# Group norms with one late product, the first output's weights by identity products, and a last image with its own buffers

## The chip, the core and the metric

The kernel runs on one core of a Trainium2 chip. Its time is the device time of one execution in microseconds (us), the median of the runs shown; lower is better. The engines are named as in the profile: PE is TensorE, DVE is VectorE, ACT is ScalarE, POOL is GpSimd, SP is SyncE. Each engine has its own queue and takes its instructions strictly in order; between engines semaphores do the ordering.

## What is computed

```python
def reference(x, ...):                      # x: 16 images, 128 channels, 64 x 64
    x = x + conv(gn(x), g_pos, g_neg, bias, input_factor, output_factor)
    x = x + attention_free(gn(x), Wq, Wk, Wv, B, Wm)
    return x

def conv(x, ...):
    v = round(clip(x * input_factor, -1, 1) * 127) / 127 * 0.6
    v = pad(swap the last two axes of v)
    fv = patches3x3(v + 0.1 * v ** 3)
    outs = [fv @ (g_pos - g_neg)[i] for i in range(3)]
    y = adc(outs[2]) + 4 adc(outs[0]) + 2 adc(outs[1]) + adc(outs[2])
    return y * output_factor + bias

def attention_free(x, ...):                 # 64 inner channels
    q, k, v = Wq x, Wk x, Wv x
    return Wm (q * (exp(B) (exp(k) v)) / (exp(B) exp(k)))

def gn(v):                                  # 32 groups of 4 channels, over the whole image
    return (v - mean) / sqrt(var + 1e-5)
```

Everything is float32; `adc` rounds to an integer and clips.

## The kernel before

**Work.** Channels lie on the 128 partitions, one image after the other. The 3x3 convolution goes through a transformed domain: DVE forms transformed rows of the quantized image (`gr`, `er`, `pa`, `pb`, `cs`, `cq`, `cd`, `p0`, `p5`, `e0`, `e5`), PE multiplies them with transformed weights, ACT and DVE carry the results back. Each image has three outputs (i = 0, 1, 2, the three weight planes), each in two halves, so there are six half-blocks, .0 to .5. A half-block holds eight products of `Block.half` (`q1`, `q2`, `q0`, `q3` for two points u) and later five of `Block.rest` (`P`, two in each of `o0` and `o1`). Between them stand ACT copies out of PSUM: `m1` (L579) before `q2`, `sd` (L581) before `q0` and `q3`, `sA` (L584) after `q0`. DVE adds with `Bo`, `df`, `sm`, `ma`, `mc`, `S0`, `S3` and `bc` (L625), ACT rounds with `tk` (L633), DVE clips with `bA`/`bB` (L636), and a POOL DMA adds the output into the integer tile `acc` with `aA`/`aB` (L643).

**The second layer.** Class `End` makes the residual: ACT writes `acc` times a scale with a row sum (`cx0` to `cx3`, L699), POOL DMAs add the input image onto it (`cd0x` to `cd3x`, L702), ACT squares with a row sum (`sq0` to `sq3`, L364). Then comes the group norm, and four `Pair`s of 1024 columns: normalize (`xn`), three projections (`kp`, `vp`, `qp`), `ek`, `ekv`, the mixing product `dn`, a reciprocal (`g`, `u`, `ln`, `ex`), `oa`, `ob`, `oc`, the output product `op`, `r`, a POOL DMA adding the residual (`rd`, L812) and the store (`st`, L813). The pairs' normalized tile and their output `r` share two buffers `xns`.

**Group norm** (class `Norm`). Per image there is one for the input (name x) and one for the residual (name y). Per channel it takes a sum and a sum of squares about a shift, which `shift` (L357 or L360) makes from the channel's own first quarter. `begin` (L368 to L378) makes the channel's mean and spread, `means` multiplies the mean with a group-averaging matrix `grp2` on PE (L383), `squares` (L387 to L389) adds what the channel's mean differs from the group's, `variances` averages again on PE (L392), and `guess`, `root`, `finish` make 1/sqrt. That is two products that depend on each other, both after the last square.

**Weights.** In the first 20 us the three weight planes are loaded as g_neg, negated (`W0a` to `W2a`, L313) and g_pos added by POOL DMAs (`W0A` to `W2A`, L240). Then each plane is transformed into `us` by fifteen small DVE and ACT operations (`Wic` to `Wip`, L316 to L333).

**Order.** The order on all five queues is written out in lists of names: `FIRST` for the start and the first two images, `ORDER` once per turn for the middle images (a turn holds the convolution of image p and the second layer of images p-1 and p-2; "+1" means the work belongs to the turn before), and `LAST` for the last two images. The names are the keys of the dictionaries that `operations` returns.

**The last image.** `Last` finishes half-blocks .4 and .5 of image 15: `tP`, `tp`/`to` are the products (into `pb` and `py`), `tbc`/`tbd` DVE sums in PSUM (L625), `tk0`/`tk3` ACT roundings (L633), `tb` clips, `ta` additions into `acc` (L684). The input image is loaded by SP into `x2e` (L717), and `tx` (L724) makes acc times scale plus input with row sums, `ts` (L364) the squares; then the norm and four `LastPair`s with buffers of their own.

Of the kernel before, what the change touches and what calls it, by code (L numbers as in the profile page):

```python
# [30 lines left out]
EPS = 1e-5  # L31

RECIP = float(0x7EF311C7)
RSQRT = float(0x5F3759DF)
# [28 lines left out]
    hs0+2 x0+2 hq0+2 hs1+2 hq1+2 hq2+2 hq3+2 W0a+2 W0A+2 hs2+2 hs3+2 xa+2 W1a+2 pmx+2 xb+2  # L63
    pvx+2 W2a+2 xc+2 xl+2 hi+2 xd+2 W0b+2 W0c+2 hn1+2 hn0+2 W0e+2 W2A+2 hc0+2 hc1+2 W0d+2 W0f+2
    hn3+2 W2f+2 li0+1 hc3+2 hr1+2 hv1+2 hr0+2 hv0+2 li1+1 W2c+2 W0j+2 er0+2 hn2+2 W0g+2 W1A+2
    sx0+1 sx1+1 W0i+2 gr0+2 W0J+2 cp+2 W0k+2 hc2+2 hr3+2 W1c+2 W0h+2 W1b+2 x0+1 hr2+2 hv3+2
    W1e+2 W1J+2 hv2+2 W0n+2 W0l+2 hb+2 er1+2 sy1+1 W1f+2 gr1+2 W1j+2 li3+1 W0m+2 W0p+2 W0o+2
    pb1+2 hz1+2 hz0+2 sy0+1 li2+1 sx2+1 sy2+1 hcs1+2 hcs0+2 q11.0+1 hcq1+2 hcq0+2 pa1+2 sx3+1
    q10.0+1 sy3+1 m11.0+1 xa+1 W1d+2 W2b+2 hcd0+2 q21.0+1 cs1+2 m10.0+1 W1g+2 q20.0+1 sd0.0+1
    sd1.0+1 W2d+2 hcd1+2 lj0+1 W1h+2 q01.0+1 q30.0+1 q00.0+1 W2e+2 W2g+2 W1i+2 sA1.0+1 cd1+2  # L70
    sA0.0+1 pmx+1 W2h+2 q31.0+1 q11.1+1 m11.1+1 xb+1 cq1+2 q10.1+1 W1l+2 m10.1+1 q21.1+1 lj1+1
    Bo.0+1 W2J+2 pvx+1 W2j+2 q20.1+1 sd0.1+1 q00.1+1 sd1.1+1 q01.1+1 W1k+2 q30.1+1 df.0+1 xc+1
    W1m+2 q31.1+1 p0+1 xl+1 W1o+2 W1n+2 xd+1 sA0.1+1 e0+1 n1+1 P.2+1 sm.0+1 q10.2+1 W1p+2 W2i+2
    Bo.1+1 W2l+2 n0+1 sA1.1+1 df.1+1 q11.2+1 m10.2+1 q20.2+1 sd0.2+1 cl0+1 q00.2+1 sm.1+1
    m11.2+1 ma.2+1 q21.2+1 sA0.2+1 sd1.2+1 q10.3+1 mc.2+1 q01.2+1 p5+1 s0+1 cl1+1 S0.2+1
    q30.2+1 q31.2+1 va0+1 s1+1 S3.2+1 sA1.2+1 lj3+1 W2m+2 q11.3+1 W2n+2 m10.3+1 Bo.2+1 bc.2+1
    m11.3+1 q20.3+1 bA.2+1 va1+1 df.2+1 q21.3+1 lj2+1 e5+1 sd0.3+1 sd1.3+1 n3+1 o1.2+1 n2+1
    o0.2+1 q00.3+1 gr0+1 q30.3+1 q31.3+1 sA0.3+1 q01.3+1 tk.2+1 P.3+1 W2p+2 li0+0 er0+1 sA1.3+1
    W2o+2 q10.4+1 Bo.3+1 sm.2+1 cp+1 bc.3+1 df.3+1 q11.4+1 m11.4+1 o0.3+1 cl2+1 cl3+1 W2k+2
    sx0+0 sm.3+1 s2+1 va2+1 mc.4+1 ma.4+1 q21.4+1 m10.4+1 q20.4+1 sd0.4+1 o1.3+1 sd1.4+1 S0.4+1  # L80
    aA.2+1 x0+0 q30.4+1 li1+0 tk.3+1 S3.4+1 q00.4+1 sA0.4+1 q31.4+1 P.4+1 bc.4+1 s3+1 q01.4+1
    q10.5+1 Bo.4+1 o1.4+1 bB.3+1 va3+1 sx1+0 bA.4+1 er1+1 m10.5+1 q20.5+1 sA1.4+1 aA.4+1 sy1+0
    q11.5+1 m11.5+1 o0.4+1 gr1+1 sd0.5+1 li3+0 tk.4+1 sy0+0 q21.5+1 P.5+1 q00.5+1 sd1.5+1
    q01.5+1 df.4+1 pb0+1 sA1.5+1 q30.5+1 sA0.5+1 q31.5+1 bc.5+1 pa0+1 o1.5+1 Bo.5+1 cq0+1
    df.5+1 cs0+1 o0.5+1 li2+0 tk.5+1 P.0+0 q10.0+0 sm.4+1 m10.0+0 q11.0+0 m11.0+0 sm.5+1
    q20.0+0 sd0.0+0 q21.0+0 sd1.0+0 cd0+1 q01.0+0 mc.0+0 aB.3+1 S0.0+0 bB.5+1 bc.0+0 sx2+0
    pa1+1 ma.0+0 pb1+1 q00.0+0 sA0.0+0 q30.0+0 o0.0+0 S3.0+0 o1.0+0 sy2+0 q31.0+0 aB.5+1 cs1+1
    sx3+0 sy3+0 bA.0+0 aA.0+0 tk.0+0 P.1+0 sA1.0+0 q11.1+0 q10.1+0 m10.1+0 lj1+0 bc.1+0 o0.1+0
    Bo.0+0 m11.1+0 cq1+1 lj0+0 xa+0 o1.1+0 tk.1+0 cd1+1 bB.1+0 aB.1+0 q20.1+0 sd0.1+0 pmx+0
    xb+0 ho+2 q21.1+0 p5+0 sd1.1+0 q00.1+0 pvx+0 xc+0 q01.1+0 p0+0 sA0.1+0 df.0+0 q10.2+0  # L90
    sA1.1+0 q11.2+0 q30.1+0 xl+0 q31.1+0 m10.2+0 q20.2+0 m11.2+0 e5+0 e0+0 cx0+0 Bo.1+0 y0+0
    cx1+0 sm.0+0 cx2+0 sd0.2+0 df.1+0 cd0x+0 cx3+0 q21.2+0 cd1x+0 cd2x+0 q00.2+0 xd+0 sd1.2+0
    sm.1+0 mc.2+0 q01.2+0 sA0.2+0 n1+0 n0+0 q30.2+0 ma.2+0 sq0+0 cd3x+0 S0.2+0
"""
START = "x0 xa pmx xb pvx xc xl xd gr0 er0 cp gr1 er1 pb1 pa1 cs1 cq1 cd1"

LAST = """
    cl0+2 sA1.2+2 S3.2+2 q31.2+2 lj3+2 st2+2 q10.3+2 cl1+2 P.2+2 bc.2+2 m10.3+2 q11.3+2 m11.3+2
    s0+2 q20.3+2 q21.3+2 o0.2+2 Bo.2+2 va0+2 s1+2 va1+2 sd0.3+2 o1.2+2 bA.2+2 sd1.3+2 q01.3+2
    sq1+2 sq2+2 lj2+2 gr0+2 sq3+2 q30.3+2 q00.3+2 tk.2+2 sA1.3+2 er0+2 q31.3+2 sA0.3+2 ya+2  # L100
    df.2+2 n3+2 n2+2 pmy+2 yb+2 P.3+2 bc.3+2 Bo.3+2 cp+2 q11.4+2 pvy+2 q10.4+2 yc+2 cl3+2
    df.3+2 o0.3+2 m10.4+2 m11.4+2 o1.3+2 q20.4+2 q21.4+2 yl+2 s3+2 yd+2 xn0+2 sd0.4+2 sd1.4+2
    kp0+2 vp0+2 sm.3+2 tk.3+2 P.4+2 q01.4+2 cl2+2 sm.2+2 ek0+2 va3+2 mc.4+2 s2+2 st3+2 aA.2+2
    S0.4+2 ekv0+2 bc.4+2 dn0+2 sA1.4+2 g0+2 q00.4+2 sA0.4+2 va2+2 u0+2 xn1+2 ln0+2 o1.4+2 gr1+2
    o0.4+2 q30.4+2 oa0+2 ex0+2 kp1+2 er1+2 tk.4+2 qp0+2 ob0+2 vp1+2 q11.5+2 ma.4+2 oc0+2 S3.4+2
    ek1+2 m11.5+2 pb0+2 op0+2 r0+2 ekv1+2 q31.4+2 Bo.4+2 rd0+2 q10.5+2 pa0+2 m10.5+2 st0+2
    P.5+2 q20.5+2 df.4+2 bc.5+2 sd0.5+2 q21.5+2 sd1.5+2 dn1+2 q00.5+2 g1+2 bB.3+2 xn2+1 bA.4+2
    q01.5+2 q30.5+2 o1.5+2 o0.5+2 u1+2 cs0+2 oa1+2 ln1+2 cd0+2 q31.5+2 ex1+2 tk.5+2 sA1.5+2
    sA0.5+2 cq0+2 aB.3+2 sm.4+2 kp2+1 qp1+2 vp2+1 ob1+2 ek2+1 aA.4+2 Bo.5+2 oc1+2 q10.0+1 op1+2
    m10.0+1 q20.0+1 r1+2 q11.0+1 m11.0+1 P.0+1 sd0.0+1 df.5+2 sm.5+2 ekv2+1 mc.0+1 S0.0+1  # L110
    q21.0+1 dn2+1 bB.5+2 q00.0+1 bc.0+1 o1.0+1 o0.0+1 rd1+2 g2+1 u2+1 sA0.0+1 ln2+1 aB.5+2
    sd1.0+1 ma.0+1 st1+2 q30.0+1 oa2+1 ex2+1 ob2+1 tk.0+1 xn3+1 pb1+2 S3.0+1 q01.0+1 bA.0+1
    qp2+1 oc2+1 pa1+2 kp3+1 op2+1 r2+1 vp3+1 ek3+1 cs1+2 cq1+2 ekv3+1 q31.0+1 P.1+1 bc.1+1
    q10.1+1 m10.1+1 sA1.0+1 Bo.0+1 df.0+1 rd2+1 dn3+1 o0.1+1 g3+1 u3+1 oa3+1 ln3+1 ex3+1 o1.1+1
    tk.1+1 q11.1+1 q20.1+1 cd1+2 aA.0+1 qp3+1 m11.1+1 bB.1+1 q21.1+1 sd0.1+1 q00.1+1 ob3+1
    sm.0+1 oc3+1 op3+1 sd1.1+1 aB.1+1 sA0.1+1 r3+1 q30.1+1 cx1+1 p0+1 e0+1 rd3+1 q01.1+1 cx0+1
    sA1.1+1 q31.1+1 Bo.1+1 q10.2+1 m10.2+1 df.1+1 q11.2+1 q20.2+1 cd1x+1 p5+1 y0+1 cd0x+1 P.2+1
    cx2+1 cd2x+1 m11.2+1 sd0.2+1 q21.2+1 q00.2+1 cx3+1 sd1.2+1 q01.2+1 q30.2+1 sA0.2+1 sq0+1
    sm.1+1 q10.3+1 mc.2+1 S0.2+1 q31.2+1 cd3x+1 bc.2+1 e5+1 o0.2+1 ma.2+1 sq1+1 o1.2+1 S3.2+1
# [24 lines left out]
def conv_preact_kernel(  # L144
# [193 lines left out]
    class Norm:  # L338
# [43 lines left out]
        def means(self):  # L382
            pe.matmul(self.banks[0][:, 0:1], grp2, self.all, start=True, stop=True)  # L383
# [574 lines left out]
```

## Time and profile before

| | us |
|---|---|
| median of 3 runs (1597.41 to 1602.0) | 1597.85 |
| the profiled execution, its own time | 1598.49 |
| span of its instructions | 1596.8 |
| ACT busy | 1183.0 (74%) |
| POOL busy | 224.0 (14%) |
| mean granted TensorE clock | 0.981 |

The profiled execution is 0.64 us above the median, and 1.7 us of it lie outside the span. PE and DVE are the two engines that are nearly always busy; both are shown in the prediction. The convolution of the first image begins at 46.48 us. The shift operation of the input norm (L357) recurs from 100.28 to 1327.8 us in thirteen turns, that is every 94.4 us.

### The profile page before, as it was taken

To read this page: it belongs to the slowest core of one execution; us is meant where nothing else is said; L and a number is where in the kernel's file an instruction comes from. 1 tells how busy PE (TensorE), PEld (TensorE's weight loads), DVE (VectorE), ACT (ScalarE), POOL (GpSimd) and SP (SyncE) were. 2 spreads that over 40 slices of the span, in tenths; PEclk is the share of its full clock that TensorE was granted. 3 is DMA by queue.
4 is the path that set the end of the run, shared out by engine and by line. 5 is a ranking of instruction groups with operands and counts; after the bars stand their busy time and mean duration, and the time that the engine had idled before them with its cause. 6 is when DMAs were issued, how large, how long until landed. Compare 5 with 4: busy or idle time off the path is not lost.

```text
span 1596.8 us, 14936 instructions
## 1 busy us (share of the span) xinstructions
PE 1487.7 (93%) x4680; PEld 563.4 (35%) x4680; DVE 1479.8 (93%) x1919; ACT 1183.0 (74%) x1857; POOL 224.0 (14%) x250
## 2 busy tenths in 40 slices
PE   1798999999999999999999999999999999999985
PEld 0233433333333333333333343333333333333321
DVE  7999999999999999999999999999999999998775
ACT  7656878787777878778787877878778787766655
POOL 2001011121201112020111201111120111202010
PEclk6899999999999999999999999999999999999998
DMA  6235467594746758465684746659474675836462
GB/s 186 79 92 120 103 160 171 126 204 114 148 128 164 184 119 196 120 137 141 150 205 109 156 131 150 166 132 203 117 152 132 156 176 121 196 66 119 119 158 80
DMA packets 67361, 227.03 MB, mean 142 GB/s; under 512 B 7632, under 2 KB 8272, under 8 KB 67280
## 3 DMA queue, kind: packets, MB, share of 16 engines
q0 software_dynamic: 37904, 123.42, 42.1%
q1 hardware_dynamic: 29088, 101.59, 17.9%
q10 hardware_dynamic: 288, 1.05, 0.2%
q8 instruction: 37, 0.61, 0.2%
q14 instruction: 44, 0.36, 0.1%
HBM read 102.30 MB, written 33.55 MB: 85 GB/s over the span
## 4 chain that ended last, share of the span: by engine, by line
PE 58%; DMA 14%; issue 11%; DVE 11%; ACT 5%; POOL 2%; DVEq 0%; POOLq 0%; ACTq 0%; SPq 0%
PE py L556 19%; PE pa L556 18%; DMA x<-in_x_dram 5%; PE pz L749 5%; PE pb L556 5%; PE pz L759 3%; PE py L749 3%; DMA s<-s 3%; DMA acc<-y 3%; PE py L771 3%; ACT x L699 2%; DVE acc L610 1%; ACT gs L364 1%; DVE y L610 1%; DVE s L615 1%
## 5 line engine op out<-in xcount | busy, mean ns | idle before, releaser
L556 PE MATMUL py<-v,ud 128*128 128x512 f32 x760 | 357.0, 608 | 1.9 <-DVE py L625 1.3
L556 PE MATMUL pa<-cs,us 128*128 128x512 f32 x384 | 199.1, 620 | 41.7 <-DVE cs L514 31.9
L556 PE MATMUL pa<-cd,us 128*128 128x512 f32 x384 | 203.9, 622 | 11.7 <-ACT pb L581 11.7
L556 PE MATMUL pa<-cq,us 128*128 128x512 f32 x384 | 198.1, 612 | 11.3 <-ACT d L579 11.2
L556 PEld LDWEIGHTS py<-v,ud 128*128 128x128 f32 x760 | 138.9, 189 | 184.0 <-issue 148.9
L556 PE MATMUL pb<-cd,us 128*128 128x512 f32 x384 | 194.5, 602 | 1.9 <-ACT pb L581 1.7
L579 ACT ACTIVATE d<-pa 128x512 f32<-128x512 f32 x192 | 112.2, 594 | 37.8 <-PE pa L556 28.0
L812 POOL DMA_DIRECT2D xn<-x x60 | 59.9, 998 | 567.8 <-ACT xn L782 567.5
L581 ACT ACTIVATE pb<-pa 128x512 f32<-128x512 f32 x192 | 112.5, 586 | 31.3 <-PE pa L556 30.7
L584 ACT ACTIVATE s<-pa 128x512 f32<-128x512 f32 x192 | 110.4, 591 | 32.0 <-PE pa L556 29.9
L749 PE MATMUL pz<-xn,w 128*64 128x512 f32 x480 | 121.8, 607 | 1.3 <-ACT xn L796 1.2
L587 DVE SCALAR_TENSOR_TENSOR s<-d,pb 128x1024 f32<-128x1024 f32 x96 | 117.2, 1221 | 3.6 <-PE pb L556 3.2
L643 POOL DMA_DIRECT2D acc<-y x62 | 68.5, 1105 | 360.8 <-DVE y L636 212.2
L588 DVE TENSOR_TENSOR d<-s 128x1024 f32<-128x1024 f32 x96 | 117.5, 1224 | 1.6 <-ACT s L584 1.5
L633 ACT ACTIVATE y<-py 128x1024 int16<-128x1024 f32 x63 | 84.0, 1334 | 46.0 <-PE py L556 44.8
L782 ACT ACTIVATE xn<-py,scalars 128x512 f32<-128x512 f32 x120 | 76.0, 685 | 56.1 <-PE py L771 56.0
L556 PEld LDWEIGHTS pa<-cs,us 128*128 128x128 f32 x384 | 66.3, 191 | 139.6 <-issue 67.0
L556 PEld LDWEIGHTS pa<-cq,us 128*128 128x128 f32 x384 | 68.0, 190 | 119.5 <-issue 69.4
L556 PEld LDWEIGHTS pa<-cd,us 128*128 128x128 f32 x384 | 66.4, 190 | 123.6 <-ACT pb L581 56.9
L556 PEld LDWEIGHTS pb<-cd,us 128*128 128x128 f32 x384 | 70.2, 190 | 96.0 <-issue 85.2
L556 PE MATMUL py<-sv,ud 128*128 128x512 f32 x190 | 97.7, 596 | 3.3 <-ACT y L633 3.2
L596 POOL DMA_DIRECT2D s<-s x48 | 45.9, 956 | 339.5 <-DVE d L588 127.9
(224 smaller groups left out, 2651.8 us busy)
## 6 DMA issues: line engine op xcount, KB each, us to landing
xc<-in_x_dram SPq DMA_DIRECT2D x121, 512.0 KB, 5.6
acc<-y POOLq DMA_DIRECT2D x62, 512.0 KB, 5.5
x<-in_x_dram POOLq DMA_DIRECT2D x60, 512.0 KB, 10.4
xn<-x POOLq DMA_DIRECT2D x60, 512.0 KB, 4.9
out_dram<-xn SPq DMA_DIRECT2D x60, 512.0 KB, 5.1
s<-s POOLq DMA_DIRECT2D x48, 512.0 KB, 6.3
gmat<-in_x_dram SPq DMA_DIRECT2D x5, 512.0 KB, 8.9
x<-in_g_neg_dram SPq DMA_DIRECT2D x2, 576.0 KB, 11.4
```

The costliest lines, as they stand in the source:

```text
L556: pe.matmul(o if len(r.shape) == 2 else o.rearrange("p (t w) -> p t w", w=W2), w, r, start=start, stop=stop, skip_group_check=True,)
L579: f"m1{u}.{k}": lambda u=u, a=a: act.activation(d[:, u], a, AF.Copy),
L581: f"sd{u}.{k}": lambda a=a, b=b: act.activation(b, a, AF.Copy, scale=-1.0),
L584: f"sA{u}.{k}": lambda u=u, a=a: act.activation(s[:, u, 0], a, AF.Copy),
L587: f"Bo.{k}": lambda: dve.scalar_tensor_tensor(s[:, :, 1], d, 2.0, pb, ALU.mult, ALU.add),
L588: f"df.{k}": lambda: dve.tensor_tensor(d, s[:, 1], s[:, 0], ALU.subtract),
L633: act.activation(self.column(self.part(1)[0], h), y, AF.Copy)
L643: pool.dma_start(a, y, accum_op=ALU.add)
L749: pe.matmul(self.tiles(o)[h * IC : (h + 1) * IC], w, x[:, t[0] : t[1] : t[2]], start=True, stop=True)
L759: pe.matmul(o[c, t], eb[r, c], self.half(x)[r, t], start=True, stop=True, skip_group_check=True)
L782: act.activation(g[:, t], self.tiles(self.op[h]), AF.Identity, bias=bias_sb)
L812: "rd": lambda: pool.dma_start(self.r, self.x2, accum_op=ALU.add),
```

## The change

1. **Group norms.** The shift is now the group's: the first part's means (`first`) are averaged over the group by an early product (`common`, `pkx`/`pky`), and `shift` (`xz`/`yz`) makes from it the shift of the squares and an exact offset. The sums of both kinds then refer to one number for the whole group, so that one product of two columns (`means`) gives mean and negative variance at once. EPS is put into a fifth column of the sums by POOL memsets. Per norm two products remain, one of them early.
2. **The first output's weights.** For plane 0 the sums of scaled planes are made by PE: products with 1, -1, 2, -2 and 4 times the identity (`diag`) accumulate in the PSUM tile `pz` (`W0q`, `W0s`, `W0u`), and ACT copies them out with a scale (`W0r`, `W0t`, `W0v`). The DVE operations `W0c`, `d`, `e`, `f`, `h`, `i`, `l`, `o`, `p` and the ACT operations `W0b`, `g`, `m` go.
3. **The last image.** ACT writes `acc` times scale early (`Lc`), before the third output is there; POOL DMAs add the input onto it (`Lx`); `tx` adds the third output to it, so that the four `ta` go. The products `tP` fill both columns of the PSUM tile, and DVE's `tk` (`complete`) reads PSUM, adds and rounds in one operation, so that `tbc` and `tbd` go and ACT's two roundings become DVE's. The second half's products use `pz` in place of `pb`. Pairs 2 and 3 of image 14 have their normalized tile and output in `f`.
4. **The lists** `FIRST`, `ORDER` and `LAST` are written anew throughout; all names of the steps above change their places.

```diff
+    diag = x2f[:, 27 * C : 32 * C].rearrange("p (k n) -> p k n", n=P)
...
+    for k, a in enumerate((-1.0, 2.0, -2.0, 4.0)):
+        act.activation(diag[:, k + 1], diag[:, 0], AF.Copy, scale=a)
...
+        def combine(o, terms):
+            for n, (d, t) in enumerate(terms):
+                pe.matmul(o, d, t, start=n == 0, stop=n == len(terms) - 1, skip_group_check=True)
+        def rows(c, d):
+            for k in range(2):
+                o = pz[:, k, 0 : 3 * C].rearrange("p (y o) -> p y o", o=C)
+                combine(o, ((one, g0), (d[k], g1), (c, g2)))
+        def taken(p, scale):
+            copy(u[:, p : p + 2, 0:3].rearrange("p q y o -> p q (y o)"), pz[:, :, 0 : 3 * C], AF.Copy, scale=scale)
+        def along():
+            for k in range(2):
+                o = pz[:, k].rearrange("p (q o) -> p q o", o=C)
+                combine(o, ((one, u[:, :, 0]), ((one, minus)[k], u[:, :, 1]), (one, u[:, :, 2])))
...
+        def common(self):
+            pe.matmul(self.bank[:, 0:1], grp2, self.near, start=True, stop=True)
+        def shift(self):
+            c = self.bank[:, 0:1]
+            if self.add is None:
+                dve.tensor_scalar(self.sh, c, -UNIT, None, ALU.mult)
+                dve.tensor_scalar(self.ex, c, -1.0, None, ALU.mult)
...
         def begin(self):
+            dve.tensor_reduce(self.tot, self.sums, AX.X, ALU.add)
+            dve.scalar_tensor_tensor(t, t, 1.0 / HW, self.off, ALU.mult, ALU.add)
         def means(self):
-            pe.matmul(self.banks[0][:, 0:1], grp2, self.all, start=True, stop=True)
+            pe.matmul(self.bank[:, 0:2], grp2, self.tot, start=True, stop=True)
-        def squares(self):
...
-        def variances(self):
...
         def guess(self):
+            dve.tensor_copy(self.m, self.bank[:, 0:1])
+            dve.scalar_tensor_tensor(v, self.m, self.m, self.bank[:, 1:2], ALU.mult, ALU.subtract)
...
+        def complete(self, h, y):
+            t = self.d[0] if h else ss[1][:, 1]
+            dve.tensor_tensor(self.column(self.part(1)[0], h), y, t, ALU.add)
...
-                o[f"ta{r}"] = lambda r=r: dve.tensor_tensor(acc[:, r], acc[:, r], self.value(r), ALU.add)
...
-        def load(self, q):
-            sp.dma_start(self.x2[q], rows(x, self.b, q))
+        def early(self, q):
+            a = acc[:, :, 4 * q : 4 * q + 4].rearrange("p r t w -> p t r w")
+            act.activation(self.x2[q].rearrange("p (t r w) -> p t r w", t=4, r=4), a, AF.Copy, scale=ofs)
...
+                    pair.xn = f.rearrange("p r w -> p (r w)")[:, bass.ts(p - 2, CH)]
+                    pair.r = pair.xn
```

In `FIRST` the start now reads `hs0 x0 pkx xz hq0 hq3 hq1 hs2 hq2 W0a ... W0q ... W0r ... W0s ... W0t ... W0u ... W0v ... pkx ... xz`, and then the first products of the convolution; in `ORDER` the place that the prediction speaks of reads before and after:

```text
before: q01.1 sA0.1 p0 r3 q10.2 sA1.1 e0 pmx df.0 p5 q30.1 rd3 q31.1 m10.2 cx0 e5 xb pvx sm.0 cx1 q11.2 y0 Bo.1 q20.2
after:  sA0.1 q01.1 q30.1 r3 p5 sA1.1 aB.1 cx0 xa e5 y0 sm.0 q31.1 Bo.1 q10.2 pky cx1 rd3 yz m10.2 q11.2 q20.2
```

and the end of image 15's third output in `LAST`, as it is now:

```text
g2 Lc0 Bo.4 u2 ln2 oa2 qp2 kp3 df.4 ex2 sm.4 sd0.5 ob2 vp3 Lc1 Lx1 sd1.5 ek3 oc2 op2 q30.5 ekv3 dn3 Lc2 q01.5 r2 g3
q31.5 q00.5 u3 qp3 oa3 tP1 sA1.5 Bo.5 Lx0 ln3 ex3 ob3 Lx2 tp0 sA0.5 Lc3 Lx3 df.5 oc3 op3 sm.5 tma tp1 r3 tmc tP0 to1
tb1 tb2 tS0 tS1 tx1 tx2 tsh to0 tk3 tpk tsz ts1 ts2 tk0 tb3 tb0 tx0 tx3 ts0 rd3 ts3 tna tpm tnb tnl tnd
```

## The prediction

> **What bounds the kernel now.** I read the totals first, then the busy time stretch by stretch, since an average over start, middle and end says little.
>
> ```profile
> core 0: us, PE busy (x) PEld busy (x) DVE busy (x) ACT busy (x) POOL busy (x), PEclk, DMA share, GB/s
> 0.00:50.00 50.00, 9.71 (x16) 4.15 (x17) 38.04 (x66) 33.66 (x61) 9.57 (x18) 0.65 0.58 174
> 50.00:100.00 50.00, 44.44 (x99) 17.67 (x98) 49.83 (x64) 32.48 (x54) 1.68 (x2) 0.98 0.26 69
> 400.00:500.00 100.00, 97.41 (x318) 36.70 (x317) 95.05 (x122) 77.21 (x122) 13.89 (x15) 1.00 0.66 153
> ...
> 1535.00:1565.00 30.00, 16.98 (x60) 6.16 (x60) 24.31 (x43) 13.37 (x22) 1.69 (x2) 0.88 0.50 124
> 1565.00:1597.00 32.00, 22.46 (x128) 6.61 (x128) 15.84 (x24) 16.53 (x24) 1.69 (x2) 0.87 0.35 99
> ```
>
> There are three stages. From 20 to about 130 us DVE never rests (49.83 of 50): the start is DVE's, and PE waits for it. In the middle PE is busy 97 to 98%, DVE 95%: PE bounds, with some 2.3 us of idle in a turn of 94.4 us. From 1535 us nobody is full: chains of dependent steps set the time. Next, whom PE waits for in the middle (200 to 1400 us), in sum over 13 turns:
>
> ```profile
> PE pa L556 <- ACT d L579: 9.5, 14, 2.1
> PE pa L556 <- ACT s L584: 7.5, 10, 1.0
> PE pa L556 <- ACT pb L581: 5.6, 12, 0.5
> PE pz L392 <- DVE x L389: 3.4, 13, 0.3
> ```
>
> Last, the order of time on PE at both ends:
>
> ```profile
> 4.58 3.71 PE L270 MATMUL pb<-d,grp 128*128 128x512 f32 x4 [4.58 <-POOL grp L254]
> 8.12 1.88 PE L270 MATMUL py<-d,grp 128*128 128x512 f32 x4
> ...
> 46.48 3.78 PE L556 MATMUL pa<-cs,us 128*128 128x512 f32 x4 [31.85 <-DVE cs L514]
> 50.05 3.08 PE L556 MATMUL pa<-cq,us 128*128 128x512 f32 x4
> ...
> 1531.67 1.02 PE L556 MATMUL pa<-cd,us 128*128 128x512 f32 x2
> ...
> 1550.21 3.78 PE L556 MATMUL py<-v,ud 128*128 128x512 f32 x8 [1.33 <-DVE py L625]
> 1561.41 0.58 PE L383 MATMUL pa<-y,grp 128*128 128x1 f32 x2 [7.42 <-DVE y L378]
> ```
>
> The reader should see that each float32 product is two instructions, 0.86 us a pair when warm, about twice that after a rest (3.71 for four); that PE stands still from 14.6 to 46.48; and that 32.2 us pass from the last transformed product (ends about 1532.7) to the first normalized column (1564.87).
>
> **The start.** Taken away on DVE: six operations at a pitch of 0.47 (L317 to L324) and three at 0.60 (L329, L332, L333), 4.6 us while DVE bounds. But something is put in front. `pkx` stands on PE behind the L270 products, which end at 10.0, and `xz` stands on DVE ahead of three of the four sums. So the first square starts at 10.8 and not 7.16; four squares at 1.28 end at 15.9 (before 12.7). `W0a` and `W2a` (1.06 and 1.18) follow on ACT ahead of `xl`, and `xd` ends near 19.2 (16.8 before). DVE's dense work began at 19.86, so 0.6 is gained here. Then `hc0`, `hv1`, `hv0` and `W2f` wait for ACT's `hn0`, `hr1`, `hr0` and for `W2A`: about 2.5 us of rests, where before there were none. From `W2f` at about 25.2 DVE has 16.8 us of work up to `xz` of image 1: 42.0.
>
> `xz` waits for `pkx`, which stands behind the new weights. `W0A` is issued at 17.3 (14.09 before) and lands 5.8 later, 23.1. `W0q` is 12 instructions of 384 columns: cold 0.70, warm 0.32 each. The L270 rows warm up after 3.7 us, the 46.48 rows only after some 6.5, so 6 to 8.4 us. `W0s` 3.9, `W0u` 12 x 0.43 = 5.2, three ACT copies 0.9 + 0.9 + 1.2, hand-overs 1.2, `pkx` 0.4: `xz` gets its number between 42.5 and 45.0. I take 43.2, by the L270 rows, because they too start from rest. With 0.4 for `xz` and 0.6 for `hcs0` the convolution begins at 44.2. It is ahead of 46.48, but DVE is then 0.8 us behind in other work (`hz1`, `pb1`, `hcs1` not done; `p0` and two of W1 and W2 done instead): 46.42 - 45.0 = 1.4. The norms of images 0 and 1 add some 0.6 in four small operations fewer. Start: -2, from -6 (no rests) to +5 (each cold burst at the slower rows, and `W2A` late).
>
> [...]
>
> **The middle.** Per image the norms lose three DVE operations (x 13 to 12, y 15 to 13) at a pitch of 0.195: 0.6 us. PE's products stay 2 + 2. The rest is the new order. (a) The wait of the second product, 3.4 in 13 turns, goes. (b) `pky` is new on PE and needs the sum of `cx0`, which needs `aB.1` landed. In the turn at 703 us `o1.1` ends at 703.3; clip, POOL issue and a landing of about 5 give 711.0 in a usual turn. After `o1.1` PE now has `q20` to `q10.2`, up to 711.8; `cx0` (1.25) and two small operations bring `pky` to 712.75: 0.95 idle. Then `q20.2` and `q21.2` wait 0.3 and 0.2 for ACT (`cx1`, `cx2`): 1.4. Before, this place costs 9.5/13 + 3.4/13 = 1.0. So (a) and (b) together are between -1.0 (the DMA lands by 710) and +1.4 a turn (it lands 1 us later); I take +0.2, that is +2.6 in 13 turns. Behind `pky` the whole of PE is queued, and everybody waits for PE. (c) The 0.6 on DVE counts only as far as PE waits for DVE by way of ACT: nothing to 0.6 a turn, I take half: -3.8. (d) After the last square the y norm has about 1.5 us less chain to `xn0`; ACT waits there 6.8 us in 12 places (the wait of L796 on L413), the steps behind it are covered by products, so I take 0.15 a turn: -2. (e) The other places of the order, 7.5 + 5.6 in 13 turns, may close or open: I take 0, and bound them by -9 and +9. The kinds of neighbours on PE are practically the same in both lists (conv beside conv 50 and 49 times). Middle: -3.2, from -12 to +11.
>
> **The end.** Moved ahead of the last transformed product `q00.5` are `qp2`, `kp3`, `vp3`, `op2`, `dn3`: 0.93 x 3 + 1.05 + 1.02 = 4.9, so this product ends at 1537.5. From there on DVE's queue decides. After `sA0.5` (+0.7): `df` 1.14, `oc3` 0.6, `sm` 1.14, `tma`, `tmc` 2.5, two clips 0.7, `tS0`, `tS1` 2.3, two `tx` 2.56, `tsh` 0.35, `tk3` 1.24, `tsz` 0.4, `tk0` 1.24, two clips 0.7, two `tx` 2.56 = 17.4. Then `ts3` 1.3 and the norm: 0.4 + product 0.6 + four operations 0.8 + two on ACT 0.5 + 0.45 = 2.75. Sum 22.2 against 32.2. (Gone: two `bc` of 1.22, four `ta` of 0.6, ACT's `tk` and one product in the chain. New: two `tk` on DVE.) PE's own queue needs 12.9 to `tpk`, DVE asks at 13.2: just hidden. The last `Lx` is issued 2 us after `sA0.5` and must land before `tx1` at +8.4. L702 took 6.6 to 15.2; the DMAs are quiet here, so I take 7.5, a wait of 1.0, between 0 and 7. In front of `q00.5`, `Lc0` on ACT waits for `aB.5`, with `ln2`, `ex2` and `sd0.5` behind it and `op2` and `q30.5` behind those: 1 to 3 us on PE, I take 1.5. So -10 + 4.9 + 1.0 + 1.5 = -2.6. The final pairs are a latency chain in a slightly better order (`Kp2`, `Kp3` earlier, `Rd1` later): -0.7, between -2 and +2. The own buffers of pairs 2 and 3 remove rests of ACT for the store (0.62 and 1.42), counted in the 32.2. End: -3.3, from -9 to +6.
>
> [...]
>
> **The sum.** -2 - 3.2 - 3.3 = -8.5 on the profiled execution's 1598.49: 1590.0. Its own median is 0.64 lower: 1589.4, forecast **1589.5**.
>
> **The rivals.** 0.3% is 4.8 us, about what a measurement of this kernel can tell from no change: faster is below 1593.1, slower above 1602.6.
>
> *The new wait at `pky`* (slower). One product in PE's queue waits for a DMA in every turn. It decides from the point where middle idle grows by more than 0.8 us a turn, which needs `aB.1` to land some 1 us later than I put it. At +1.4 a turn: 13 x 1.4 = 18, with (c), (d) and both ends at -11: +7, 1605. For it: in the turn at 703 the landing was at 712.6, and PE rested 2.14 at L579. Against it: ACT waited for `acc` only 5.3 us in all of the middle. Chance 0.17.
>
> *The gains are taken back at the ends.* PE as a weight maker is cold and late, `xz` holds DVE (+4), the last `Lx` holds `tx1` for 5 (+1): with the middle -3.2 about 1599.5. For it: the cold rows at 46.48. Against it: 4.6 us of DVE work are really gone. Chance 0.17.
>
> *The order closes most rests.* Of 29 us that PE rests in the middle, 12 go: 1581. For it: the chain of each norm is shorter everywhere. Against it: cover between dependent products hardly changes. Chance 0.25.
>
> The forecast keeps 0.41, with 1584 to 1595 its own range. Faster: 0.37 + 0.25 + 0.02 = 0.64; same 0.19; slower 0.17. The range is 1577 to 1603.
>
> **What would show it.** Start: the first `cs` product near 44, `xz` of image 1 with an idle DVE before it. Middle: the wait at L392 gone, one at L412 on DVE's `near` in its place, about 1 us a turn; period 94.2. End: from the last `cd` product to the first L848 into `cd` 23 to 24 us; idle DVE before the first L776. The prediction is wrong if the period moves by more than 0.7 us, or if the first product stays at 46 or later.

## The result and the profile after

| | before | after |
|---|---|---|
| median, us (4 runs each) | 1599.92 (1597.41 to 1602.8) | 1637.92 (1634.94 to 1642.12) |
| ratio, 95% interval | | 1.023 (1.0205 to 1.0254) |
| span of the profiled execution, us | 1596.8 | 1640.4 |

The change makes the kernel 38 us slower; 1589.5 was forecast, with 1577 to 1603 as its range. The profiled execution of the changed kernel took 1642.12, the longest of its four, so the differences between the profiles below add up to 43.6 and not to 38. The three stages are told apart by one landmark that both kernels have: `cx0`, ACT's first conversion of an image's finished integer sums, which can begin when the transfer `aB.1` has landed. It occurs 15 times, once for every image but the last.

| span of the profiled execution, us | before | after | difference |
|---|---|---|---|
| up to the first `cx0` | 147.6 | 156.0 | +8.4 |
| from one `cx0` to the next, mean of 14 | 94.44 | 97.37 | 14 x 2.93 = +41.0 |
| from the last `cx0` to the end | 127.1 | 121.2 | -5.9 |

The middle is the loss, the end a gain, the start a smaller loss. The same rows as before the change, busy time by stretch (length, then PE, PEld, DVE, ACT, POOL, then granted clock, DMA share, GB/s):

```profile
0.00:50.00 50.00, 26.44 (x53) 12.35 (x54) 32.75 (x53) 30.44 (x54) 10.94 (x29) 0.81 0.50 144
50.00:100.00 50.00, 44.34 (x85) 16.94 (x86) 44.83 (x60) 32.16 (x56) 1.68 (x2) 0.85 0.35 100
400.00:500.00 100.00, 96.39 (x311) 37.29 (x310) 91.20 (x116) 75.54 (x119) 15.27 (x21) 0.97 0.62 144
1578.00:1608.00 30.00, 22.04 (x76) 8.27 (x71) 23.02 (x37) 15.76 (x24) 6.00 (x7) 0.89 0.83 182
1608.00:1640.00 32.00, 21.96 (x128) 6.64 (x128) 16.68 (x29) 17.15 (x26) 1.69 (x2) 0.82 0.35 99
```

In the middle PE is still at 96% and yet does less: its granted clock is 0.97 there, where it was 1.00, and DVE has gone from 95 to 91. The same columns for twelve whole turns, from the second `cx0` to the fourteenth, first before and then after:

```profile
240.01:1372.89 1132.88, 1106.40 (x3505) 418.78 (x3504) 1082.90 (x1393) 881.26 (x1381) 167.15 (x181) 1.00 0.64 151
254.11:1424.52 1170.41, 1123.33 (x3504) 428.00 (x3504) 1070.37 (x1356) 884.89 (x1381) 166.93 (x228) 0.98 0.62 146
```

Of the 37.5 us that these turns grew by, PE is idle for 20.6 more (47.1 instead of 26.5), and for 16.9 more it is busy with as many products, which ran longer. So waits are little more than half of the loss. In the start DVE, which hardly rested before from 50 to 100 (49.83), now rests 5.2 us. Whom PE waits for between 200 and 1400 us (sum, times, longest), all of its waits:

```profile
PE pz L412 <- DVE y L409: 42.2, 12, 3.9
PE py L602 <- ACT acc L679: 1.2, 7, 0.2
PE py L823 <- DVE ekv L861: 0.4, 1, 0.4
```

One place has taken nearly all: `pky`, the product that the prediction named, 3.5 us a turn; the places where PE waited before have closed. To see what it waits for, one turn in order of time (start, length, engine, what it does, in brackets the idle time before it and what ended it):

```profile
1215.26 7.23 SPq L475 DMA_DIRECT2D xc<-in_x_dram  x2
...
1220.91 1.13 ACT L429 ACTIVATE xc<-xc,x 128x1024 f32<-128x1024 f32 x1
1221.52 1.19 POOL L689 DMA_DIRECT2D acc<-y  x1 [8.28 <-DVE y L682]
1224.03 0.90 POOL L642 DMA_DIRECT2D s<-s  x1 [1.33 <-PE py L823]
1229.54 1.15 ACT L750 ACTIVATE x<-acc,scalars 128x1024 f32<-128x1024 int16 x1 [3.75 <-DMA acc<-y]
1230.81 0.16 DVE L407 SCALAR_TENSOR_TENSOR y<-y,x 128x1 f32<-128x1 f32 x1 [5.03 <-ACT x L750]
1231.08 1.21 DVE L633 SCALAR_TENSOR_TENSOR s<-d,pb 128x1024 f32<-128x1024 f32 x1
1231.22 0.38 PE L412 MATMUL pz<-y,grp 128*128 128x1 f32 x2 [3.60 <-DVE y L409]
```

`aB.1` (L689) is issued at 1221.52 and ACT starts `cx0` (L750) at 1229.54, when it has landed: 8.0 us. Three engines stand meanwhile: ACT 3.75, DVE 5.03 (with `Bo.1`, L633, behind `y0`), PE 3.60. Before the change the same step took 5.0 to 5.2 in eleven of the 13 turns and ACT waited in five only. So the question is less why PE waits there than why the transfer needs 3 us longer. The trace has two candidates beside it. One is the SP row: it covers two loads of `xc`, and its end, 1222.49, is the issue of the second (`lj0`), which had to wait for the square L429 (`sy2`, 1220.91 to 1222.04) to free the buffer; that load moves while `aB.1` moves. The other is `sm.0` (L642), issued at 1224.03.

The end, in the same view:

```profile
1585.15 1.02 PE L602 MATMUL pa<-cd,us 128*128 128x512 f32 x2
...
1596.66 1.28 DVE L776 SCALAR_TENSOR_TENSOR gmat<-y,scalars,gmat 128x1024 f32<-128x1024 int16 x1 [1.19 <-DMA gmat<-in_x_dram]
...
1599.47 0.38 PE L412 MATMUL pa<-y,grp 128*128 128x1 f32 x2 [0.39 <-DVE y L409]
1607.15 0.59 PE L438 MATMUL pa<-y,grp 128*128 128x2 f32 x2 [7.30 <-DVE y L435]
...
1609.58 2.37 ACT L848 ACTIVATE cd<-gmat,y 128x1024 f32<-128x1024 f32 x2 [0.48 <-DVE y L457]
```

From the end of the last transformed product (1586.17) to the first normalized column (1609.58) are 23.4 us, where it was 32.2.

And the start on PE:

```profile
8.17 3.16 PE L280 MATMUL py<-d,grp 128*128 128x512 f32 x4
11.17 0.28 PE L412 MATMUL pz<-x,grp 128*128 128x1 f32 x2
...
24.05 5.97 PE L324 MATMUL pz<-s,x 128*128 128x384 f32 x12 [6.22 <-DMA s<-in_g_pos_dram]
...
30.92 4.14 PE L324 MATMUL pz<-s,x 128*128 128x384 f32 x12 [0.90 <-ACT us L333]
37.20 7.11 PE L324 MATMUL pz<-us,x 128*128 128x512 f32 x12 [2.14 <-ACT us L333]
45.49 0.38 PE L412 MATMUL pz<-x,grp 128*128 128x1 f32 x2 [1.17 <-ACT us L348]
46.78 1.13 PE L602 MATMUL pa<-cs,us 128*128 128x512 f32 x2 [0.92 <-DVE cs L560]
```

### The profile page after: what moved, and what is told of

It is laid out like the page before. It is cut to its first block, busy times and chain, and to the rows that moved or that the text cites. A ratio compares the mean times of both kernels' runs of the same rounds, so it can differ in the third digit from the quotient of the medians.

```text
span 1640.4 us, 14942 instructions
## 1 busy us (share of the span) xinstructions
PE 1529.6 (93%) x4720; PEld 584.5 (36%) x4720; DVE 1457.4 (89%) x1858; ACT 1188.8 (72%) x1863; POOL 229.8 (14%) x321
## 4 chain that ended last, share of the span: by engine, by line
PE 54%; DVE 14%; issue 13%; DMA 11%; ACT 7%; POOL 1%; DVEq 0%; POOLq 0%; SPq 0%; ACTq 0%
PE pa L602 19%; PE py L602 16%; DMA acc<-y 7%; PE pz L801 5%; PE pb L602 5%; PE pz L811 3%; PE py L801 2%; PE py L823 2%; DVE acc L656 2%; ACT x L750 2%; ACT n L496 2%; DMA s<-s 2%; DVE d L634 2%; DVE py L671 1%; DVE s L633 1%
## 5 line engine op out<-in xcount | busy, mean ns | idle before, releaser
L602 PE MATMUL pa<-cs,us 128*128 128x512 f32 x384 | 210.2, 650 | 9.3 <-ACT s L630 4.9
L602 PE MATMUL pa<-cq,us 128*128 128x512 f32 x384 | 206.0, 641 | 2.1 <-ACT d L625 1.9
L630 ACT ACTIVATE s<-pa 128x512 f32<-128x512 f32 x192 | 110.9, 591 | 31.7 <-PE pa L602 21.3
L625 ACT ACTIVATE d<-pa 128x512 f32<-128x512 f32 x192 | 110.5, 591 | 25.8 <-PE pa L602 18.1
L864 POOL DMA_DIRECT2D xn<-x x58 | 49.6, 854 | 548.6 <-ACT xn L834 543.6
L689 POOL DMA_DIRECT2D acc<-y x62 | 72.5, 1170 | 338.0 <-DVE y L682 310.2
L801 PE MATMUL pz<-xn,w 128*64 128x512 f32 x464 | 117.3, 605 | 0.0
L633 DVE SCALAR_TENSOR_TENSOR s<-d,pb 128x1024 f32<-128x1024 f32 x96 | 116.9, 1217 | 0.3 <-PE pb L602 0.3
L602 PE MATMUL py<-sv,ud 128*128 128x512 f32 x192 | 107.9, 646 | 5.4 <-ACT y L679 3.3
L602 PEld LDWEIGHTS pa<-cq,us 128*128 128x128 f32 x384 | 72.2, 200 | 109.1 <-issue 56.9
L750 ACT ACTIVATE x<-acc,scalars 128x1024 f32<-128x1024 int16 x60 | 68.2, 1137 | 50.8 <-DMA acc<-y 50.8
```

The lines of the kernel that those rows point to most:

```text
L602: pe.matmul(o if len(r.shape) == 2 else o.rearrange("p (t w) -> p t w", w=W2), w, r, start=start, stop=stop, skip_group_check=True,)
L625: f"m1{u}.{k}": lambda u=u, a=a: act.activation(d[:, u], a, AF.Copy),
L630: f"sA{u}.{k}": lambda u=u, a=a: act.activation(s[:, u, 0], a, AF.Copy),
L633: f"Bo.{k}": lambda: dve.scalar_tensor_tensor(s[:, :, 1], d, 2.0, pb, ALU.mult, ALU.add),
L689: pool.dma_start(a, y, accum_op=ALU.add)
L750: act.activation(o, a, AF.Copy, scale=ofs, accum_out=self.sums[:, 0, q : q + 1])
```

## The experiments

Three theories for the middle. A: PE and DVE are held because `pky` and `y0` stand in their queues ahead of work that could go on. B: ACT, held at `cx0`, is enough to hold everybody. C: the transfer `aB.1` lands late because the load `lj0` moves beside it, and that load goes out when `sy2` has run, which the new order puts late. The table has the landmarks of every profiled run; the sections give what each was to show. Each ratio is to executions of the kernel before taken beside that run, so it can differ a little from the quotient of the medians shown. "Issue to `cx0`" is the usual turn's.

| run | median, us | ratio to before (95%) | first `cx0` | per image | last `cx0` to end | issue to `cx0` |
|---|---|---|---|---|---|---|
| before | 1599.92 | | 147.6 | 94.44 | 127.1 | 5.1 |
| changed kernel | 1637.92 | 1.023 (1.0205 to 1.0254) | 156.0 | 97.37 | 121.2 | 8.0 |
| product later | 1670.05 | 1.0441 (1.0412 to 1.0469) | 152.6 | 99.65 | 121.3 | 8.0 |
| product and `cx0` later | 1645.37 | 1.0283 (1.0257 to 1.0308) | 151.9 | 97.90 | 121.1 | 8.0 |
| early square | 1603.55 | 1.0024 (1.0008 to 1.004) | 151.7 | 94.91 | 121.4 | 5.1 |
| early square, product later | 1627.78 | 1.0163 (1.0136 to 1.019) | 154.1 | 96.47 | 120.8 | 5.1 |
| before, square late, load early | 1596.88 | 0.9989 (0.9973 to 1.0005) | 148.5 | 94.23 | 126.5 | 5.1 |
| before, load late | 1628.85 | 1.0183 (1.0154 to 1.0213) | 148.0 | 96.19 | 126.6 | 8.0 |
| norm and end in the old order, mixed last list | 1598.82 | 0.9989 (0.9975 to 1.0003) | 148.6 | 94.47 | 125.7 | 5.1 |
| norm and end in the old order | 1589.88 | 0.9941 (0.9922 to 0.9959) | 148.0 | 94.27 | 121.5 | 5.1 |
| and weights on PE | 1593.17 | 0.9964 (0.9951 to 0.9977) | 151.6 | 94.30 | 121.3 | 5.1 |
| and DVE's two rests taken out | 1594.71 | 0.9961 (0.9945 to 0.9976) | 149.6 | 94.16 | 121.6 | 5.1 |
| early square, zeros late | 1602.56 | 1.0013 (1.0 to 1.0025) | 154.1 | 94.83 | 122.0 | 5.1 |
| early square, weights on DVE, `W0l` too early | 1606.77 | 1.0038 (1.0026 to 1.005) | 154.2 | 95.00 | 121.0 | 5.1 |
| early square, weights on DVE | 1607.95 | 1.0051 (1.0032 to 1.007) | 153.5 | 95.04 | 121.4 | 5.1 |
| early square, `W2f` later | 1604.08 | 1.0032 (1.0019 to 1.0044) | 153.2 | 94.76 | 121.6 | 5.1 |

### The place of the product, and of the sum

The repeated order, the parts that move:

```
- sA1.1 aB.1 cx0 xa e5 y0 sm.0 q31.1 Bo.1 q10.2 pky cx1 rd3 yz m10.2 q11.2 q20.2 ... df.1 ... q21.2
+ sA1.1 aB.1 cx0 xa e5 sm.0 q31.1 Bo.1 q10.2 cx1 rd3 m10.2 q11.2 q20.2 ... df.1 y0 ... q21.2 pky yz
```

> The changed kernel with y0 behind df.1 and pky and yz behind q21.2 in the repeated order, nothing else. Theory A (PE and DVE are held by pky and y0, which stand in their queues before cx0 can be done): the wait of L412 falls from 3.6 us a turn to below 0.5, the time per image from 97.4 to about 94.8, in all some 1602 us. Theory B (ACT's cx0, held by the late landing of aB.1, is enough to hold everybody, because m10.2 stands behind it): the wait moves from L412 to q20.2 (PE pa L602 on ACT d L625), 2 to 3 us a turn, and the time stays above 1625. Both: issue to cx0 stays near 8 us.

The second run puts `cx0 cx1` behind `m10.2` too.

> As the run with the later product, and cx0 and cx1 behind m10.2 on ACT as well, as the kernel before has it. Theory B: now nobody is held, the time per image falls to 94.3 to 95, some 1600 in all, though the landing still takes 8 us. Theory A alone: no more than 2 us below the run with the later product.

Both were slower than the changed kernel, by 32 and by 7 us, so A's forecast (1602) fell, and so did B's for the second (1600). B's sign for the first was there: the rest at `pky` went to the products behind `m10.2`.

```profile
PE pa L602 <- ACT d L625: 47.0, 12, 4.3
PE pa L602 <- ACT s L630: 21.7, 24, 1.7
```

In the second run PE's wait for L625 stayed at 47.1 in 13 turns (200 to 1450 us): with `m10.2` let through, `m11.2` behind `cx0` and `cx1` is next. In all three orders something on the way to PE is behind the late transfer. The issue to `cx0` stayed at 8 us in both, whatever stood behind.

### The load

```
- m10.1 Bo.0 ... ob3 ... oc3 sy2 df.0
+ m10.1 sy2 Bo.0 ... ob3 ... oc3 df.0
```

> The changed kernel with one square of the next input (sy2) moved on ACT from behind tk.1 to behind m10.1, so that the load lj0 which it releases is issued some 10 us earlier. Theory C (aB.1 lands 3 us late because that load moves beside it): issue to cx0 falls from 8 to about 5.2 us, the wait of L412 from 3.6 to about 1 us a turn, the time per image to 94.7, some 1602 in all, with the product where the change put it. If something else makes the landing late (sm.0, or the transfer as such): issue to cx0 stays at 7.5 to 8.4 and the time above 1630.

```profile
805.22 3.94 SPq L475 DMA_DIRECT2D xc<-in_x_dram  x2
...
812.20 1.19 POOL L689 DMA_DIRECT2D acc<-y  x1 [9.00 <-DVE y L682]
814.53 0.90 POOL L642 DMA_DIRECT2D s<-s  x1 [1.15 <-PE py L823]
...
817.29 1.15 ACT L750 ACTIVATE x<-acc,scalars 128x1024 f32<-128x1024 int16 x1 [1.06 <-DMA acc<-y]
818.97 0.38 PE L412 MATMUL pz<-y,grp 128*128 128x1 f32 x2 [0.91 <-DVE y L409]
```

This is the order of time in one turn of that run. Both loads have been issued by 809.16, 3 us before `aB.1`; `sm.0` still follows 2.3 us behind it, as in the changed kernel. The transfer now takes 5.1, so it was the load and not `sm.0`. (By the distance to `aB.1` the load goes out 4 us earlier than in the changed kernel, not the expected 10.) PE's wait at L412 fell from 42.2 us in 12 turns to 16.1 in 13, the clock in the stretch from 400 to 500 us returned from 0.97 to 1.00, and 34 of the 38 us came back by moving one square of 1.2 us on an engine that is not full. The other direction was tried on the kernel before: one square late, nothing else of the change.

> The kernel before, with nothing of the change but the place of one square: sy2 on ACT behind tk.1 and sd0.1 (and xa, which needs it, behind p0 on DVE), so that the load lj0 is issued beside aB.1. Theory C (the load beside the transfer makes it land late): issue to cx0 goes from 5.1 to about 8 us, ACT waits some 3 us a turn at cx0, time per image from 94.6 to 96.5 or more, in all 1620 to 1645. If the lateness needs the new norm or the new order of the rest: issue to cx0 stays at 5 to 6, within 1597 to 1606.

That edit left `lj0` ahead of `sy2` in the list. So the load went out before the square (which then read other data than it should), and its issue to `cx0` stayed at 5.1, its time at 1596.88, ratio 0.9989 (0.9973 to 1.0005): it doesn't test C by itself. The edit again, with the load behind the square:

```
- q10.1 sy2 P.1 ... q21.1 qp3 lj0 bB.1 sd0.1 sd1.1 xa aB.1 ... sA0.1 p0 r3
+ q10.1 P.1 ... q21.1 qp3 bB.1 sd0.1 sy2 lj0 sd1.1 aB.1 ... sA0.1 p0 xa r3
```

> The kernel before with sy2 behind sd0.1 on ACT, lj0 behind sy2 in the list (in the run with the late square it had been left ahead of it, so that the load went out early and overwrote what the square reads), xa behind p0. Theory C: issue to cx0 from 5.1 to about 8 us, ACT waits about 3 us a turn at cx0, in all 1620 to 1645. If the lateness needs the new norm or the rest of the new order: 1597 to 1606.

```profile
1187.77 12.91 SPq L428 DMA_DIRECT2D xc<-in_x_dram  x2
...
1199.10 1.13 ACT L363 ACTIVATE xc<-xc,x 128x1024 f32<-128x1024 f32 x1
1199.71 1.19 POOL L642 DMA_DIRECT2D acc<-y  x1 [7.13 <-DVE y L635]
...
1207.58 1.15 ACT L698 ACTIVATE x<-acc,scalars 128x1024 f32<-128x1024 int16 x1 [2.86 <-DMA acc<-y]
...
1211.62 1.89 PE L555 MATMUL pa<-cq,us 128*128 128x512 f32 x2 [2.54 <-ACT d L578]
```

With the old norm, the old order of everything else and no product at that place, the late load (issued by 1200.68) brings 7.9 us from issue to `cx0` in this turn, 1.75 us an image and 30 us by the medians (the profiled execution, 1622.9, is the fastest of four). The two runs differ in the place of `lj0` alone: the late square by itself costs nothing (94.23 an image, 5.1 to `cx0`), the late load costs the rest. C is shown in both directions.

With the transfer in time, the product's place was tried again.

> The run with the early square, and y0 behind df.1, pky and yz behind q21.2 as well. If the product's place is what is left in the middle: the rest at L412 (16.1 us in 13 turns there) goes, time per image 94.9 to some 94.0, in all 1592. If PE then waits for m10.2 behind cx0 instead, as in the run with the later product: the rest moves to L625's d and the time stays at 1602 or above.

It got 24 us slower than the run with the early square. The rest at L412 went to L625 and L630 (18.9 and 16.4 us, 200 to 1400 us). The part at L625 is what the second half of the expectation named, products behind `m10.2` and `m11.2`, which stand behind `cx0` to `cx2` on ACT. For the part at L630 the order of time in one turn suggests a reason:

```profile
836.65 0.28 PE L412 MATMUL pz<-y,grp 128*128 128x1 f32 x2
836.97 0.22 DVE L421 TENSOR_SCALAR y<-pz,scalars 128x1 f32<-128x1 f32 x1 [1.45 <-PE pz L412]
838.56 0.21 DVE L456 SCALAR_TENSOR_TENSOR x<-x,scalars 128x1 f32<-128x1 f32 x1
839.06 2.56 ACT L496 ACTIVATE n<-xc,x 128x1024 int16<-128x1024 f32 x2 [0.93 <-DVE x L457]
841.51 0.58 ACT L630 ACTIVATE s<-pa 128x512 f32<-128x512 f32 x1
842.15 1.13 PE L602 MATMUL pa<-cs,us 128*128 128x512 f32 x2 [1.12 <-ACT s L630]
```

DVE stands at `yz` (L421) for the product, the input norm's `xd` (L456) is behind it, ACT waits for `xd` before its quantization (L496), `sA0.2` (L630) is behind that, and PE waits for it. The edit had put `yz` ahead of `sm.1` and `xd`, at a point where its product was not done: a product that is moved back needs its reader moved to where the number is ready. No run moved `yz` alone, so this is a reading and not shown. In the old order below (product behind `q21.2`, `yz` behind a later `df.1`) PE has no wait there at all.

### Norm and end alone

The order of the kernel before for start and middle, the first image's weights on DVE, the new norm's steps put where nothing reads late, the zeroing products of L280 behind `pmx` of image 0:

```
- q20.5+1 ... sy1 ... oa1+1 ... q00.5+1 ex1+1 tk.5+1 ob1+1 ... xb pvx ... xc ... q21.2 ... df.1
+ q20.5+1 ... oa1+1 ... q00.5+1 pkx ex1+1 tk.5+1 ob1+1 xz sy1 ... xb ... q21.2 pky ... df.1 yz
```

> The order of the kernel before for the start and the middle, first image's weights on DVE as before, with the new norm (pkx behind q00.5, pky behind q21.2, yz behind df.1) and the new end; the zeroing products of L280 behind pmx of image 0. If the order and not the norm is what costs: time per image 94.0 to 94.8, some 1590 in all (1583 to 1600). If a norm with its product ahead of the squares costs as such, wherever it stands: over 1605.

The middle came as expected (94.47), the whole did not: 1598.82. Its last list was a mixture (the old one up to the last image's pairs, the rest of the new one), and from the last `cx0` to the end it needs 125.7 us. With the changed kernel's last list whole:

> The run with the norm and the end (order of the kernel before, new norm), with the changed kernel's whole last order, from the last two images on, in place of the mixed one. From that run's profile: first cx0 at 148.6, 14 images at 94.5, and from the last cx0 121.4 as in the run with the early square: 1592 to 1593. If the new end needs the new order in the images before it: 1597 or more.

It is the fastest version here, 0.9941 (0.9922 to 0.9959) of the kernel before; the only others whose interval lies below 1 are the two below that are built on it. Its gain is the end: 127.1 to 121.5. In the middle new norm and old order give 0.17 us an image, no more than these two runs with the same middle differ (94.47 and 94.27). The waits of PE there are at the places of the kernel before, with none at L401, its `pky`; but the one for `d` has grown from 9.5 to 17.4 us, more than the wait of the second product (3.4) that went:

```profile
PE pa L591 <- ACT d L614: 17.4, 13, 2.9
PE pa L591 <- ACT s L619: 11.4, 13, 1.1
PE pa L591 <- ACT pb L616: 3.1, 12, 0.5
```

### The start

Two single undoings, both on the run with the early square. First the products of L280, put behind the first norm:

```
+ def zeros(): for o in (pb[:, 0], pb[:, 1], py[:, 0], py[:, 1]): pe.matmul(o, grp2, ds[0][:, 0], ...)
- hs0+2 x0+2 pkx+2 ... pmx+2 hi+2
+ hs0+2 x0+2 pkx+2 ... pmx+2 hm+2 hi+2
```

> The run with the early square, with the four zeroing products of L280 behind pmx of image 0 instead of ahead of its pkx. If these products delay the start: first square near 7.9 (11.68 in the changed kernel), W0A issued near 14.3 (18.10), the weights' first products warm, first transformed product at 43 to 44, in all 1599 to 1600. If the weights' products on PE bound the start by themselves: first transformed product at 46 or later, 1603.

The first square came at 8.07 (11.68) and the first transformed product at 44.74 (46.23 in the run with the early square), but the first `cx0` at 154.1: no gain. (Five profiles with one and the same start list, the changed kernel's, have their first `cx0` between 151.7 and 156.0, so a smaller gain than that can't be read off one profile; the medians, 1602.56 and 1603.55, are within each other's scatter.) Then the weights:

> The run with the early square, with the first output's weights made on DVE and ACT as in the kernel before (the operations W0b to W0p where W0q to W0v stood). If making them on PE is what delays the start: all 1599 to 1601. If it saves what it took from DVE (nine operations, 4.6 us, some of them in rests of DVE): 1605 to 1608.

This gave 1606.77, ratio 1.0038 (1.0026 to 1.005), first product 51.87; the list had `W0l` overwrite what `W0J` and `W0j` read, so it was run again with these two ahead.

> The run with the early square and the first output's weights on DVE again, now with W0J and W0j ahead of W0l, whose output takes the place of what they read (in the first run of this edit it overwrote it). First transformed product at 50 to 52, in all 1605 to 1608, if the earlier run's time holds; 1601 or less if its extra wait made it late.

First product 51.13, 1607.95: in the changed start, weights on PE are worth some 3 to 4 us by the medians of the two runs, though the intervals of the ratios overlap. In the old start they are not:

> As the run before it, with the first output's weights made on PE (W0q to W0v) in the start's order of the kernel before. If weights on PE shorten the start where nothing else in it is moved: first transformed product 2 to 4 us earlier than there, first cx0 at 145 to 147, in all 2 to 4 us less. If DVE's saved work was never on the path up to cx0, or pkx behind the weights holds xz: first cx0 at 148 or later, no less in all.

1593.17, 3 us more than with the weights on DVE by the medians (the intervals overlap), first product 49.81 instead of 47.10. DVE's waits from 15 to 80 us have it:

```profile
DVE xn L361 <- DMA x<-in_g_pos_dram: 4.3, 1, 4.3
DVE x L414 <- PE pz L409: 4.1, 1, 4.1
```

The first is `W2f`, which now comes up before `W2A` has landed, the second `xz`, for `pkx` behind the weights on PE. Taking both out:

> The run with the order of the kernel before and the weights on PE, with W2f and W2c behind gr0 and xz of image 1 (and sy1, which needs it) behind W1f. If the saved work of DVE was eaten by its own queue, which stood 4.3 us at W2f for W2A and 4.1 us at xz for pkx behind the weights: these two rests go, first transformed product at 42 to 44 (49.81), first cx0 at 145 to 147, in all 1586 to 1588.5. If PE's or ACT's queue is late by itself: first transformed product above 47, no less than 1590.

```profile
DVE x L431 <- ACT xc L426: 3.3, 1, 3.3
DVE gmat L529 <- ACT y L493: 3.0, 1, 3.0
```

The first product came 3.9 us earlier (45.94), but DVE now waits 6.3 us for ACT's quantization (L493) and squares (L426), where the two rests had been 8.4, and the whole stays where it was. In the changed start, with `W2f` and `W2b` moved behind `gr0`:

> The run with the early square, with W2f and W2b behind gr0 in the changed kernel's own start. If DVE's rest at W2f (3.9 us there) is what the start lost: first transformed product 2 to 3 us earlier, first cx0 at 148 to 149.5, in all some 1600. If the start is held later on (a first product 1.5 us earlier had brought nothing by the first cx0 in the run with the late zeros): first cx0 at 151.5 to 154, 1602 to 1604.

No gain (1604.08); DVE's rest went to the next operation that needs a weight transfer (3.6 us at L359).

## Why the prediction was wrong

**The middle, the step that failed.** Steps (a) and (b) put the change of PE's wait at this place between -1.0 and +1.4 us a turn; it was +2.5 (42.2 us in 12 turns, 3.5 a turn, where 1.0 had been; PE's other waits closed and gave back some 0.8). The failing part is the figure inside (b), "a landing of about 5 give 711.0 in a usual turn": it is a duration of the trace before, taken over into an order in which another transfer had been moved beside it. The landing takes 8.0. The move was in the order's text: `sy2` goes from ahead of `P.1` to behind `tk.1`, and `lj0`, which it holds, is a DMA on SP. I followed the queues of PE, DVE and ACT past the new places and not SP's; step (e) put all other moves at nothing, between -9 and +9, and this one alone is worth +34 (the run with the early square). The rest of (b) held: the wait at L412 is where it was forecast, and with the landing at 5.1 it is 16.1 us in 13 turns, 1.24 a turn where 1.0 had been, which is the +0.2 that was taken. A second term was left at nothing without being named: that PE's products could run slower. With the late landing they did, at a granted clock of 0.98 in place of 1.00, and that is 16.9 of the 37.5 us in the twelve turns; with the landing at 5.1 it is 2.7 (1109.1 us busy and 1106.4).

**The rival.** *The new wait at `pky`* had place and condition right ("`aB.1` to land some 1 us later than I put it") and its price too small: it landed 3 later, PE waited 2.5 more a turn there, and its products ran slower by 1.4 a turn. That the run with the early square came to 1603.55, near this rival's 1605, is chance: its middle is 0.5 us an image over the kernel before, not 1.4, and its start is late by 4. A rival whose condition had been followed back to what else is transferred at that moment would have had the price.

**Steps (c) and (d)** (-3.8 and -2) were too large, as far as these runs can tell: new norm and old order together give 94.47 and 94.27 against 94.44, between nothing and -2.4 in 14 images. PE bounds there (busy 1106.4 of 1132.9 us in the twelve turns before), and what DVE is spared hardly reached it.

**The end** was forecast at -3.3 and came at -5.9. From the last transformed product on it is as worked out (23.4 of the forecast 23 to 24; the wait at the first L776 1.19, forecast 1.0; the final pairs -1.1, forecast -0.7). The mis-sized term is the delay of that product by the work put ahead of it: 4.9 + 1.5 forecast, from the last `cx0` to the product's end 63.0 before and 67.0 after, so 4.0. The last `Lx` landed in 7.8 us, 7.5 forecast.

**The start** was forecast at -2, from -6 to +5; it was +8.4 in this profile, and +4.1 to +6.5 in the four other profiles with the same start list. The first burst of the weights took 5.97, the low end of its forecast; the other terms fell on the late side: the second four L280 products slow (3.16, not 1.88), DVE's rests between 20 and 50 us 5.0, not 2.5 (3.78 of it at `W2f`), and the third burst of the weights slow (7.11 against 5.2), after a rest of 2.14 for ACT's `W0t`, a copy put at 0.9 in the forecast; `xz` at 45.9, not 43.2. But repairing these terms one by one moved the first product and not the first `cx0`. So the deeper fault, as far as the runs show it, is the first line of that part, that 4.6 us taken from DVE are gained "while DVE bounds": DVE was full, but its suppliers (the weight transfers, ACT) were only just ahead of it, and it came to stand at them. From the first product to the first `cx0` DVE is busy for the same time in both kernels, 99.8 of 101.1 us before and 99.9 of 109.2 after (99.9 of 105.5 with the early square): all that this stretch lost is rests of DVE. After the change they are 3.9 us for PE at L671, 1.9 for ACT's squares at L434, 1.5 for a POOL transfer at L656 and smaller ones, and PE's granted clock in the stretch is 0.91 where it was 0.97. Which move in the list brings these rests was not found; the two lists differ in nearly every place there.

## What to carry to other kernels

When an order is changed, list for every moved instruction the transfers that it releases, and see what those run beside: a load that nobody waits for can delay a transfer for which all engines wait (here from 5.1 to 8.0 us). A duration from the trace before did not hold here once a load lay beside the transfer; beside each such figure put which transfers lay next to it. Work taken from a full engine is a gain only up to the slack of its nearest supplier: in the old order the 4.6 us taken from DVE left the first `cx0` at 151.6, where it had been 148.0.

## What was not expected of the hardware

A 512 KB accumulating transfer issued by POOL took 5.0 to 5.2 us to its reader in most turns with no load from SP beside it, and mostly 7.8 to 8.4 when SP issued one of 512 KB some 0.6 us after it, in both kernels. In three turns of the changed kernel the load went out at another moment, and the delay followed it: 6.5 us when it was issued 1.1 before the transfer, 6.79 and 6.85 when 0.06 after (5.7, and 7.0 and 7.1, in the kernel before with the load late). With a load issued 3.4 before (the run with the early square) it took 5.1, and a second transfer from POOL's own queue, 2.3 us behind the first, was there too.

PE's clock: after rests of 0.90 us the twelve weight products of 384 columns ran at 4.14 us, after 2.18 (in the run with the late zeros) at 5.83. The twelve of 512 columns took 7.11 after rests of 1.90, 2.01, 2.14, 2.25 and 2.49, and 5.42 after 0.96, 1.39, 1.82 and 1.94. So the length of the rest alone doesn't decide: 1.90 (product later) was slowed and 1.94 (early square, `W2f` later) was not. In the middle, rests of 3.6 to 3.9 us were followed by slow products, sometimes at once (two pairs of 1.97 and 1.89 at 744.51 and 746.27 us, 1.02 when warm), sometimes after a first pair at speed (1.10 and then 1.85 at 1231.46 and 1232.44 us). The granted clock was 0.58 from 744 to 748 us and 0.59 from 1232 to 1236, and 1.00 in the four us ahead of each.

The busy rows of the changed kernel around its burst of 7.11, which begins at 37.20 after the rest of 2.14:

```profile
34.00:36.00 2.00, 1.05 (x4) 0.30 (x2) 1.67 (x4) 1.97 (x3) 0.00 (x0) 1.00 0.00 0
36.00:38.00 2.00, 0.80 (x2) 0.49 (x3) 2.00 (x3) 2.00 (x4) 0.00 (x0) 1.00 0.00 0
38.00:41.00 3.00, 3.00 (x5) 1.17 (x4) 3.00 (x3) 2.91 (x13) 0.00 (x0) 0.51 0.00 0
41.00:44.00 3.00, 3.00 (x8) 1.11 (x6) 3.00 (x6) 0.00 (x0) 0.00 (x0) 0.92 0.00 0
```

The granted clock is 1.00 in the rest and in the first 0.8 us of the burst, 0.51 in the next three and 0.92 in the three after: it was low behind the rest, not in it. What decides besides the length of the rest was not shown.
